# A GRU over 128 steps: the input products of steps 4 to 7 by two-level sums, other load queues, and another order of the program

## The chip, the cores and the metric

One core of a Trainium2 chip runs the whole program. The metric is the device time of one execution in microseconds (us). TensorE (PE) multiplies, VectorE (DVE), ScalarE (ACT) and GpSimd (POOL) do the elementwise work, and SP only issues DMAs; ACT and POOL issue some too.

## The reference

`x` is 64 x 128 x 512 (batch, steps, inputs), `h` is 64 x 512, all in float32. The output is `x` plus the hidden state of each step.

```python
def step(h, inp):
    x_t, prop = inp
    comb = jnp.concatenate([x_t, h], axis=-1)
    z = jax.nn.sigmoid(comb @ Wz + bz)
    r = jax.nn.sigmoid(comb @ Wr + br)
    comb2 = jnp.concatenate([x_t, r * h], axis=-1)
    h_cand = jnp.tanh(comb2 @ Wh + bh)
    h_new = (1.0 - z) * h + z * h_cand
    h_next = jnp.where(prop, jnp.tanh(h_new @ Wp + bp), h_new)
    return (h_next, h_new)
```

`prop` holds in every fourth step (t = 3, 7, ...) but the last. `Wz`, `Wr` and `Wh` are 1024 x 512: the upper half meets x (called the input half, `wx` in the kernel), the lower half meets h (`wh`). `Wp` is 512 x 512 (`wp`).

## The kernel before

The products with h must wait for h, step by step. The products with x don't: they are made ahead, in groups of four steps (group g holds steps 4g to 4g + 3), and fill PE between the products with h. Their results lie as `cp` and are added to, or copied (the line's name is a seed) into, the accumulators of a step.

*Plain products.* `plain(t)` makes the x products of steps 0 to 3. A unit is 8 products of 32 rows by 128 columns for one gate (R, Z, H) and one of the four blocks k of the inputs; there are 48. The profile counts two records for a float32 product, so that a unit is 16 records.

*Batches.* For groups 1 and up `batch(...)` makes the x products by a scheme with seven products instead of eight. A unit is 4 products of 32 x 192 (8 records). The scheme is used on two levels: the outer level has seven products, numbered 1 to 7, each made of seven inner ones (49 units a group), and needs sums of the weights (`tt`, `tw`, `tf`: `sum_inner`, `sum_outer`, all through `weigh`, 128 x 384 on POOL or 128 x 768 on DVE), sums of x between steps and input halves (`o12`, `o34`, made from the transposed x, `xT`), sums of these (`s12r`, `s4r`, `s56`, `s73`, by `four`), and, after the products, folds on POOL (`to_c`, `to_m`, `more_c`: 128 x 768 into `st` or `mb`), whose result goes by a DMA and a copy on ACT into `cp`. A batch holds two of the outer products and uses the scratch banks q, y, a and x; ACT seeds ps_q with the summed bias (`bias_s`, made on POOL) and copies banks into each other; DVE adds two blocks.

Group 1 (steps 4 to 7) is made in another way before: its outer level is an ordinary product (`special`, and `TERMS` for batches that add up two of them), 56 units in three batches, four folds; its sums of x are `s12r` and, by `sum_raw34`, the raw sums of steps 6 and 7, in the buffer of `s73`.

*Recurrent products.* `gates_plain` (steps 0, 1 and 124 to 127) multiplies h with `wh` as it is; `gates_seven` (the others) uses a seven-product scheme with sums `sa` of the transposed h, made on POOL as soon as both halves of h are there (`hT`). Then comes the candidate (products of `rhT`, the transposed r * h, with `wh_2`, into ps_e for one half of the batch and ps_r for the other), and in steps with `prop` the product with `wp`.

*Start.* PE runs 42 products of zeros (`idle`) while the first data are loaded, then the biases are spread over the partitions by products with a row of ones (`spread`, `spread_wide`). SP's queue loads x of step 0, the input halves of Wr, Wz, Wh, x of steps 4 to 7, then `wh` and `wp`. POOL's queue loads x of steps 1 to 3 and h0.

*Order.* Every operation is written into a plan with the data that it reads and writes; the table `ORDER` (a packed list) fixes the order in which the program is emitted, for all engines (`arrange`). An engine does its operations strictly in this order.

## Time and profile before

| | us |
|---|---|
| median of 3 runs | 1230.0 (1229.81 to 1231.96) |
| profiled execution, span | 1229.9 |
| PE busy | 1213.1 |
| POOL, DVE, ACT busy | 942.4, 864.0, 789.1 |
| first x product on PE begins | 9.30 |
| step 0's first product with h begins | 29.25 |
| step 4's first product with h begins | 87.75 |
| step 124's first product with h begins | 1200.45 |
| last product on PE begins | 1223.95 |

Rows of the profile read: start and length in us, engine, line of the kernel, operation, output <- input as the program names them, then sizes and the count; in square brackets the idle time of the engine ahead of the row and what ended it. `s` stands for `s73` or `s56`, `o` for `o12` or `o34`. A row's length on PE holds the way through the array too, so the distance of starts is what a product costs PE.

### The profile page before, as it was taken

To read this page: it belongs to the slowest core of one execution; us is meant where nothing else is said; L and a number is where in the kernel's file an instruction comes from. 1 tells how busy PE (TensorE), PEld (TensorE's weight loads), DVE (VectorE), ACT (ScalarE), POOL (GpSimd) and SP (SyncE) were. 2 spreads that over 40 slices of the span, in tenths; PEclk is the share of its full clock that TensorE was granted. 3 is DMA by queue.
4 is the path that set the end of the run, shared out by engine and by line. 5 is a ranking of instruction groups with operands and counts; after the bars stand their busy time and mean duration, and the time that the engine had idled before them with its cause. 6 is when DMAs were issued, how large, how long until landed. Compare 5 with 4: busy or idle time off the path is not lost.

```text
span 1229.9 us, 85504 instructions
## 1 busy us (share of the span) xinstructions
PE 1213.1 (99%) x37666; PEld 1139.7 (93%) x37666; DVE 864.0 (70%) x2831; ACT 789.1 (64%) x2305; POOL 942.4 (77%) x1489
## 2 busy tenths in 40 slices
...
GB/s 191 128 46 54 39 62 50 59 61 48 54 49 53 60 59 53 40 61 49 64 60 39 55 54 54 64 42 56 50 56 58 60 42 51 57 55 59 39 58 37
DMA packets 92754, 71.50 MB, mean 58 GB/s; under 512 B 7515, under 2 KB 88283, under 8 KB 92382
## 3 DMA queue, kind: packets, MB, share of 16 engines
...
q0 software_dynamic: 512, 0.53, 0.2%
q14 instruction: 76, 0.62, 0.2%
...
## 4 chain that ended last, share of the span: by engine, by line
PE 95%; DMA 2%; SPq 1%; issue 1%; DVE 1%; ACT 0%; POOL 0%; POOLq 0%; ACTq 0%; DVEq 0%
PE ps_e L412 16%; PE ps_r L412 16%; PE ps_b L412 13%; PE ps_y L412 12%; PE ps_q L412 12%; PE ps_x L412 12%; PE ps_z L412 10%; PE ps_a L412 6%; DMA wx<-in_L_cond_Wr_dram 0%; DMA wx<-in_L_cond_Wh_dram 0%; DMA wx<-in_L_cond_Wz_dram 0%; SPq L483 0%; DMA wh<-in_L_cond_Wr_dram 0%; SPq L538 0%; POOL st L860 0%
## 5 line engine op out<-in xcount | busy, mean ns | idle before, releaser
L1070 POOL TENSOR_TENSOR sa<-hT 128x64 f32<-128x64 f32 x244 | 76.3, 322 | 145.4 <-DVE hT L975 92.0
L412 PE MATMUL ps_z<-wh,sa 128*32 128x128 f32 x3904 | 160.8, 273 | 0.9 <-POOL sa L1070 0.9
L860 POOL TENSOR_TENSOR st<-mb,mb 128x768 f32<-128x768 f32 x77 | 141.1, 1833 | 23.0 <-ACT mb L827 18.6
L884 ACT COPY cp<-st 64x384 f32<-64x384 f32 x248 | 125.9, 509 | 25.0 <-DVE keep L1078 11.5
L412 PE MATMUL ps_e<-wh,rhT 128*32 128x128 f32 x4096 | 141.1, 273 | 0.3 <-issue 0.3
L412 PE MATMUL ps_r<-wh,rhT 128*32 128x128 f32 x4096 | 140.4, 273 | 0.7 <-DVE rhT L975 0.6
L412 PEld LDWEIGHTS ps_z<-wh,sa 128*32 128x32 f32 x3904 | 122.5, 110 | 8.7 <-issue 2.4
L412 PEld LDWEIGHTS ps_r<-wh,rhT 128*32 128x32 f32 x4096 | 121.1, 110 | 4.6 <-DVE rhT L975 1.2
L1164 POOL TENSOR_TENSOR xj<-xj,h 128x256 f32<-128x256 f32 x127 | 93.3, 735 | 40.6 <-DVE h L1147 40.3
L412 PEld LDWEIGHTS ps_e<-wh,rhT 128*32 128x32 f32 x4096 | 120.9, 110 | 2.6 <-issue 0.8
L975 DVE STREAM_TRANSPOSE hT<-h 128x128 f32<-128x128 f32 x318 | 98.0, 310 | 34.5 <-ACT h L1022 21.0
L860 POOL TENSOR_TENSOR mb<-mb,mb 128x768 f32<-128x768 f32 x60 | 110.1, 1834 | 13.0 <-ACT mb L827 12.4
L1018 ACT COPY ps_r<-cp 128x128 f32<-128x128 f32 x256 | 69.1, 270 | 56.2 <-DVE h L1147 26.5
L566 DVE STREAM_TRANSPOSE xT<-xj 128x256 f32<-128x256 f32 x128 | 83.4, 655 | 18.2 <-DMA xj<-in_x_dram 11.6
L412 PE MATMUL ps_y<-tw,s 128*32 128x192 f32 x1456 | 94.3, 326 | 0.3 <-issue 0.3
L1078 DVE TENSOR_TENSOR ps_z<-ps_z,keep 128x128 f32<-128x128 f32 x244 | 71.6, 294 | 27.4 <-PE ps_z L412 21.3
L412 PE MATMUL ps_e<-wh,hT 128*32 128x128 f32 x2144 | 86.7, 273 | 1.9 <-ACT ps_e L1018 1.8
L1078 DVE TENSOR_TENSOR keep<-ps_b,cp 128x128 f32<-128x128 f32 x244 | 67.9, 281 | 28.2 <-PE ps_b L412 27.5
L860 POOL TENSOR_TENSOR st<-mb 128x768 f32<-128x768 f32 x47 | 86.1, 1832 | 1.7 <-ACT mb L827 1.0
L1070 POOL TENSOR_TENSOR sa<-hT,sa 128x64 f32<-128x64 f32 x244 | 78.9, 323 | 9.3
L975 DVE STREAM_TRANSPOSE rhT<-rh 128x128 f32<-128x128 f32 x256 | 78.9, 309 | 6.8
L412 PE MATMUL ps_b<-wh,hT 128*32 128x128 f32 x1952 | 80.3, 273 | 0.0
...
## 6 DMA issues: line engine op xcount, KB each, us to landing
...
out_dram<-xj SPq DMA_DIRECT2D x254, 64.0 KB
xj<-in_x_dram SPq DMA_DIRECT2D x248, 64.0 KB
...
```

The source lines that it names most:

```text
L412: nc.tensor.matmul(dst, lhsT=lhsT, rhs=rhs, start=start, stop=True, skip_group_check=True)
L566: lambda: nc.vector.transpose(out=xT_(g)[:, i].rearrange("p c (a h b) -> p h (c a) b", a=S, h=S), in_=xj(t).rearrange("p h (e k) -> p h k ...
L860: el("pool", 768, lambda: nc.gpsimd.tensor_add(dst, a, b), reads, writes, rank=FOLD)
L884: el("act", 384, lambda h=h, own=own: nc.scalar.copy(cp_(2 * g + a)[own, nb, h].rearrange("p b g u -> p (b g u)"), st_(n)[own, h].rearrang ...
L975: add("dve", 0.23, lambda: nc.vector.transpose(out=dst, in_=src), reads, writes, land=0.08, main=True)
L1018: el("act", n, lambda: nc.scalar.copy(dst, src), reads, writes, "+" + bank, main=True)
L1070: tensor(lambda: nc.gpsimd.tensor_sub(sa[:, n], a, b), reads, [("sa", t, n)], n=64, engine="pool")
L1078: tensor(lambda: nc.vector.tensor_add(dst, a, b), reads, writes, used_)
L1164: el("pool", 256, lambda: nc.gpsimd.tensor_add(x_out, x_out, h_(new_)), [("h", new_, 0), ("h", new_, 1)] + xk_, xk_)
```

## The change

Six edits in one:

1. Group 1 is made as the other groups are: 49 units in four batches, (1, 2), (6, 5), (7, 3) and (4) alone, with `s12r`, `o12`, `s56`, `o34`, `s73`, `s4r` and seven folds. `special`, `TERMS` and `sum_raw34` go. The inner weight sums 6, 7 and 4 stand ahead of the batches. A batch may hold one product (W = 1).
2. In `plain`, R and Z of blocks k = 1 to 3 are made by one unit with 256 columns; k = 0 stays apart, since it opens a bank.
3. `wx` is loaded by block and gate in the order R0, Z0, R1, Z1, R2, Z2, R3, Z3, H0 to H3 (one DMA each for k = 0 and 1 of R and Z, two for the others).
4. x of steps 1 to 3 goes from POOL's queue (12 DMAs) to ACT's (6), x of steps 4 to 7 from SP's (8 DMAs between Wh's input half and `wh`) to POOL's (8).
5. In the last group the batch (3, 5) comes before (7, 4); before it was (7, 5), then (3, 4).
6. The table is new.

The diff, cut to its core, with two lines of the table:

```diff
@@ ORDER @@
 ORDER = """
-c-mEYcYIaXneE>D?0tIg_uO;ty~1`J+llR%xFzv;;xxxjb?juEHuENBGMOavUXq!~v;;Lokpu`N5CTLIh>i-95CTN+2+?~-G=b<{p!bRSy+7VvXMNvV>-)
...
+c-n2-2Y40NnK0lv(|ez}Q|`>%izGlagB>T1<HYgWj#HgD#mR2gNgn&zB>V4fc9Y#d+0FBBR)`{j=pdO65+IsDAV8vvCPW8;D57^n6}^}Lo4LXz&(523&Ue0Z
...
@@ -449,28 +427,21 @@
     def rows(ap, t, h):
         return ap[ts(h, V), t, :].rearrange("b (q j) -> q b j", q=NQ)
 
-    def load_x(t):
+    def load_x(t, name="sp"):
         for h in range(S):
-            op = load("sp", lambda h=h: nc.sync.dma_start(out=xj(t)[:, h, :], in_=rows(x, t, h)),
-                      [("xj", t, h, q) for q in range(NQ)], cost=0.585, few=True)
-            if t < 3 * Q4:
+            op = load(name, lambda h=h: queue(name).dma_start(out=xj(t)[:, h, :], in_=rows(x, t, h)),
+                      [("xj", t, h, q) for q in range(NQ)], cost=0.585 if name == "sp" else 0.45, few=True)
+            if 2 * Q4 <= t < 3 * Q4:
                 plan.behind.append((late, op.index))
 
-    def load_wx(i, k, wide=False):
+    def load_wx(i, k, pieces=1):
 
         w = gates_in[i][:D].rearrange("(p k) n -> p k n", k=K)
-        if wide:
-            load("sp", lambda: nc.sync.dma_start(out=wx[:, k, i, :], in_=w[:, k]),
-                 [("wx", 0, i, k)], size=256.0, cost=0.43)
-            return
...
+        tall = P // pieces
+        for n in range(pieces):
+            load("sp", lambda n=n: nc.sync.dma_start(out=wx[ts(n, tall), k, i, :], in_=w[ts(n, tall), k]),
+                 [("wx", 0, i, k, n)], size=256.0 / pieces, cost=0.43)
+        plan.whole(("wx", 0, i, k), [("wx", 0, i, k, n) for n in range(pieces)])
 
     def load_wh(dst, w, keys, over=(), ks=K):
 
@@ -498,46 +469,41 @@
     add("pool", 0.2, lambda: nc.gpsimd.memset(ones, 1.0), (), [("ones", 0)])
     for q in range(NQ):
         load_step(0, q, ("sp", "actq")[q % 2])
+    load_wx(R, 0)
+    load_x(1, "actq")
+    load_wx(Z, 0)
+    load_wx(R, 1)
+    load_x(2, "actq")
+    load_wx(Z, 1)
+    load_x(3, "actq")
     for i in range(3):
         load_bias(i)
-    for i in range(3):
-        for k in range(0, K, 2):
-            if i == R and k == 0:
-                load_wx(i, k, True)
-                load_wx(i, k + 1, True)
-            else:
-                load_wx(i, k)
+    for k in (2, 3):
+        for i in (R, Z):
+            load_wx(i, k, 2)
+    for k in range(K):
+        load_wx(H_, k, 2)
     add(
         "act", 1.5, lambda: nc.scalar.activation(dummy, ones[:, 0:1], AF.Sigmoid),
         [("ones", 0)], [("dummy", 0), ("row_free", 0)],
     )
-    for q in range(NQ):
-        load_step(1, q, "poolq")
-    for h in range(S):
-        for q in range(NQ):
-            load(
-                "poolq",
-                lambda h=h, q=q: nc.gpsimd.dma_start(
-                    out=steps_in[part(q), 2:4, h, :], in_=x[ts(h, V), 2:4, ts(q, J)]),
-                [("xj", t, h, q) for t in (2, 3)], size=32.0,
-            )
     for q in range(NQ):
         load(
             "poolq",
             lambda q=q: nc.gpsimd.dma_start(
                 out=h_(0)[part(q)], in_=h0[:, ts(q, J)].rearrange("(h b) j -> b h j", h=S)
             ),
-            [("h", 0, h, q) for h in range(S)], size=32.0,
+            [("h", 0, h, q) for h in range(S)], [("wx", 0, R, 1)], size=32.0,
         )
     for h in range(S):
         plan.whole(("h", 0, h), [("h", 0, h, q) for q in range(NQ)])
     for h in range(S):
         for q in range(NQ):
             load(
-                "sp",
-                lambda h=h, q=q: nc.sync.dma_start(
+                "poolq",
+                lambda h=h, q=q: nc.gpsimd.dma_start(
                     out=steps_in[part(q), Q4 : 2 * Q4, h, :], in_=x[ts(h, V), Q4 : 2 * Q4, ts(q, J)]),
-                [("xj", t, h, q) for t in range(Q4, 2 * Q4)], cost=0.47,
+                [("xj", t, h, q) for t in range(Q4, 2 * Q4)], [("wx", 0, Z, 2)], size=64.0,
             )
     for i in range(3):
         load_wh(wh[i], gates_in[i][D:], ("wh", 0, i))
@@ -740,37 +702,48 @@
-            for k in range(K):
...
-                def unit(e=e, k=k, ps=ps, slot=slot, c0=c0, s0=s0, first=first):
...
+        def products(k, gates):
...
+            def unit():
+                for h in range(S):
+                    for q in range(NQ):
+                        left = v[:, c0, s0 * B + h * V : s0 * B + (h + 1) * V]
+                        if len(gates) > 1:
+                            mm(ps[part(q), h::2], left, wx[:, k, gates[0] : gates[-1] + 1, ts(q, J)], first and h == 0)
+                        else:
+                            mm(ps[part(q), slot + h], left, wx[:, k, gates[0], ts(q, J)], first and h == 0)
...
+        products(0, [R])
+        products(0, [Z])
+        for k in range(1, K):
+            products(k, [R, Z])
+        for k in range(K):
+            products(k, [H_])
@@ -787,15 +760,16 @@
-        ps = halves
-        mb, c5, q2 = mb_(n), c5_(n), q2_(n)
+        W = len(ms)
+        ps = {b: v[:, :W] for b, v in halves.items()}
+        mb, c5, q2 = mb_(n)[:, :W], c5_(n)[:, :W], q2_(n)[:, :W]
...
-                for x_, w_ in TERMS.get(i, ((i, i),)):
-                    left, lk = lhs(g, x_, j)
-                    right, rk = factor(w_, j)
...
+                left, lk = lhs(g, i, j)
+                right, rk = factor(i, j)
...
@@ -1167,22 +1140,15 @@
             load("sp", lambda h=h: nc.sync.dma_start(out=rows(out, t, h), in_=x_out[:, h, :]),
                  [], [("xj", t, h, q) for q in range(NQ)], cost=0.585, few=True)
 
-    def special(g, a, p1, p2, p3):
-        to_c(g, a, 0, p1, p2)
-        to_c(g, a, 1, p1, p3)
-
     def sums_of(g, *at):
         plan.due = min(at) - 0.3
         for t in range(g * Q4, g * Q4 + Q4):
             join(t)
         plan.due = at[0]
         sum_raw12(g)
-        if g == 1:
-            sum_raw34(g)
-        else:
-            for due, f in zip(at[1:], (sum_s12, sum_s34, sum_raw4)):
-                plan.due = due
-                f(g)
+        for due, f in zip(at[1:], (sum_s12, sum_s34, sum_raw4)):
+            plan.due = due
+            f(g)
 
     add("pe", 0.01, lambda: None, [("bits", 0)],
         [("A", 0), ("R", 0), ("P", 0, 0), ("P", 0, 1)]
@@ -1203,15 +1169,21 @@
     sum_inner(3)
     plan.due = -0.5
     sum_outer()
-    sums_of(1, -1.0)
+    for i in (6, 7, 4):
+        plan.due = -0.4
+        sum_inner(i)
+    sums_of(1, -1.0, -0.9, -0.8, -0.7)
     batch([(1, 1), (1, 2)], 0.0, 0.8, (1, 0))
-    batch([(1, 10), (1, 11)], 0.8, 1.6, (5, 5))
-    batch([(1, 8), (1, 9)], 2.4, 0.8, (1, 0))
-    special(1, 0, 1, 2, 10)
-    special(1, 1, 8, 9, 11)
-    for due, i in ((0.5, 6), (1.0, 7), (1.5, 4)):
-        plan.due = due
-        sum_inner(i)
+    to_c(1, 0, 0, 1, 2)
+    batch([(1, 6), (1, 5)], 0.8, 0.8, (0, 5))
+    to_m(1, 6, 1)
+    n = to_c(1, 0, 1, 6, 5, True)
+    batch([(1, 7), (1, 3)], 1.6, 0.8)
+    more_c(1, 0, 1, n, 3)
+    to_m(1, 7, 6)
+    to_c(1, 1, 1, 7, 5)
+    batch([(1, 4)], 2.4, 0.4)
+    to_c(1, 1, 0, 7, 4)
 
     for k in range(KH):
         b11, b21, b12, b22 = wh[R][:, k], wh[R][:, KH + k], wh[Z][:, k], wh[Z][:, KH + k]
@@ -1246,13 +1218,22 @@
         batch([(o, 2), (o, 6)], at + 4 * L, L)
         to_c(o, 0, 0, 1, 2)
         to_m(o, 6, 1)
-        batch([(o, 7), (o, 5)], at + 5 * L, L, (0, 5))
-        n = to_c(o, 0, 1, 6, 5, True)
-        to_m(o, 7, 6)
-        to_c(o, 1, 1, 7, 5)
-        batch([(o, 3), (o, 4)], at + 6 * L, L)
-        more_c(o, 0, 1, n, 3)
-        to_c(o, 1, 0, 7, 4)
+        if o < T // Q4 - 1:
+            batch([(o, 7), (o, 5)], at + 5 * L, L, (0, 5))
+            n = to_c(o, 0, 1, 6, 5, True)
+            to_m(o, 7, 6)
+            to_c(o, 1, 1, 7, 5)
+            batch([(o, 3), (o, 4)], at + 6 * L, L)
+            more_c(o, 0, 1, n, 3)
+            to_c(o, 1, 0, 7, 4)
+        else:
+            batch([(o, 3), (o, 5)], at + 5 * L, L, (0, 5))
+            n = to_c(o, 0, 1, 6, 5, True)
+            more_c(o, 0, 1, n, 3)
+            batch([(o, 7), (o, 4)], at + 6 * L, L)
+            to_m(o, 7, 6)
+            to_c(o, 1, 1, 7, 5)
+            to_c(o, 1, 0, 7, 4)
 
     plan.due = LAST - 1.0
     load_wh(wz, Wz[D:], ("wz", 0), [("tw", 0, 5, 0), ("tw", 0, 5, 1), ("t5", 0, 5)], KH)
```

The lines of the profile move with it: a product is L412 before and L390 after, a weight sum L611 and L577, a fold L860 and L833, `sa` L1070 and L1043, a transpose of x L566 and L532, a bank copy or seed of a batch L827 and L800, the spreads L925 and L945 to L898 and L918, sums by `four` L643 to L646 to L609 to L612.

What the table does at three places (without the rows' numbers; names carry buffer numbers). PE's first products with x, behind the products of zeros; before:

```order
L925 MATMUL ps_y_114<-wt_68 32x128 x12
L412 MATMUL ps_x_113<-wx_63,xT_0_81 32x128 x8
L412 MATMUL ps_a_112<-wx_63,xT_0_81 32x128 x16
L412 MATMUL ps_x_113<-wx_63,xT_0_81 32x128 x16
L412 MATMUL ps_a_112<-wx_63,xT_0_81 32x128 x16
L412 MATMUL ps_z_107<-wx_63,xT_0_81 32x128 x8
```

and after:

```order
L390 MATMUL ps_b_108<-wx_63,xT_0_81 32x128 x8
L390 MATMUL ps_z_107<-wx_63,xT_0_81 32x128 x8
L390 MATMUL ps_b_108<-wx_63,xT_0_81 32x128 x8
L390 MATMUL ps_z_107<-wx_63,xT_0_81 32x128 x8
L390 MATMUL ps_z_107<-wx_63,xT_0_81 32x2x128 x8
L390 MATMUL ps_a_112<-wx_63,xT_0_81 32x2x128 x8
L390 MATMUL ps_x_113<-wx_63,xT_0_81 32x2x128 x8
L390 MATMUL ps_b_108<-wx_63,xT_0_81 32x2x128 x8
L898 MATMUL ps_y_114<-wt_68 32x128 x12
```

The spread of the biases (from `wt`) moves from the head of the x products behind the first 16 units' worth of them, four merged pairs (2x128) among these.

POOL up to the end of `s73`; before:

```order
L611 TENSOR_TENSOR tw_3_70<-tw_3_70 128x12x32
L1164 TENSOR_TENSOR xj_80<-xj_80,h_1_99 128x256
L643 TENSOR_TENSOR s73_0_93<-xT_1_82 128x128
L644 TENSOR_TENSOR s73_0_93<-s73_0_93,xT_1_82 128x128
L645 TENSOR_TENSOR s73_0_93<-xT_1_82 128x128
L611 TENSOR_TENSOR tt_76<-tt_76,tw_4_71 128x384
L646 TENSOR_TENSOR s73_0_93<-xT_1_82,s73_0_93 128x128
L670 TENSOR_TENSOR o12_0_96<-xT_0_81 128x256
L860 TENSOR_TENSOR st_0_88<-mb_0_85 128x2x2x192
```

and after:

```order
L646 TENSOR_TENSOR o34_0_97<-xT_1_82,o12_0_96 128x256
L1137 TENSOR_TENSOR xj_80<-xj_80,h_1_99 128x256
L577 TENSOR_TENSOR tf_3_75<-wx_63 128x384
L612 TENSOR_TENSOR s56_0_94<-o12_0_96,s56_0_94 128x128
L609 TENSOR_TENSOR s73_0_93<-o34_0_97 128x128
L612 TENSOR_TENSOR s4r_0_95<-xT_1_82,s4r_0_95 128x64
L577 TENSOR_TENSOR tt_76<-tt_76,wx_63 128x384
L833 TENSOR_TENSOR st_0_88<-mb_0_85 128x2x2x192
L577 TENSOR_TENSOR tt_76<-tt_76,tw_4_71 128x384
L611 TENSOR_TENSOR s73_0_93<-o34_0_97 128x128
L610 TENSOR_TENSOR s73_0_93<-s73_0_93,o34_0_97 128x128
L612 TENSOR_TENSOR s73_0_93<-o34_0_97,s73_0_93 128x128
```

The sums of `s73` now come from `o34`, itself a sum, and stand behind `s56`, `s4r` and the first fold into `st`.

PE at the end of step 123; before:

```order
L412 MATMUL ps_z_107<-wh_1_65,sa_0_106 32x128 x8
L412 MATMUL ps_e_109<-wh_2_66,rhT_0_103 32x128 x16
L412 MATMUL ps_z_107<-wh_1_65,sa_0_106 32x128 x8
L412 MATMUL ps_r_110<-wh_2_66,rhT_0_103 32x128 x16
L412 MATMUL ps_e_109<-wp_67,hT_0_100 32x128 x16
L412 MATMUL ps_r_110<-wp_67,hT_0_100 32x128 x16
```

and after:

```order
L390 MATMUL ps_z_107<-wh_1_65,sa_0_106 32x128 x8
L390 MATMUL ps_e_109<-wh_2_66,rhT_0_103 32x128 x16
L390 MATMUL ps_r_110<-wh_2_66,rhT_0_103 32x128 x16
L390 MATMUL ps_y_114<-tw_4_71,s4r_0_95 32x192 x4
L390 MATMUL ps_x_113<-tt_76,o34_0_97 32x192 x4
L390 MATMUL ps_x_113<-tt_76,xT_1_82 32x192 x4
L390 MATMUL ps_e_109<-wp_67,hT_0_100 32x128 x16
L390 MATMUL ps_r_110<-wp_67,hT_0_100 32x128 x16
```

Three batch units stand between the last products of `rhT` and the product with `wp`, and the product with `sa` is ahead of both products of `rhT`.

332 lines of the change are left out of this document (148 added, 184 removed).

## The prediction

> **What bounds the kernel now.** I read the page first, then a table of stages, then single engines where that table shows idle time. From the page, the busy times and the shares of the chain that ended last:
>
> ```profile
> PE 1213.1 (99%) x37666; PEld 1139.7 (93%) x37666; DVE 864.0 (70%) x2831; ACT 789.1 (64%) x2305; POOL 942.4 (77%) x1489
> PE 95%; DMA 2%; SPq 1%; issue 1%; DVE 1%; ACT 0%; POOL 0%; POOLq 0%; ACTq 0%; DVEq 0%
> ```
>
> PE is busy for all but 1229.9 − 1213.1 = 16.8 us of the span. Where those lie is told by PE's busy time in each stretch (columns: stretch, its length, busy time and records, clock, DMA share, GB/s):
>
> ```profile
> 0.00:40.00 40.00, 34.77 (x906) 1.00 0.79 199
> 40.00:60.00 20.00, 19.99 (x600) 1.00 0.30 86
> 60.00:80.00 20.00, 17.88 (x506) 1.00 0.12 31
> 80.00:1150.00 1070.00, 1068.91 (x33351) 1.00 0.21 54
> 1150.00:1200.00 50.00, 48.69 (x1558) 1.00 0.20 53
> 1200.00:1230.00 30.00, 22.82 (x788) 0.99 0.13 34
> ```
>
> From 80 to 1150 us only 1.1 us is idle: the change leaves the work of that stretch alone, so it can neither gain nor lose there. What it can move is the head (5.2 us idle before 40), two stalls between 60 and 80 (2.1), and the last 80 us (8.5). PE's timeline of the head and of those stalls, in order of time:
>
> ```profile
> 6.00 1.69 PE L925 MATMUL ps_y<-wt 1*32 1x128 f32 x24
> 9.30 1.08 PE L412 MATMUL ps_x<-wx,xT 128*32 128x128 f32 x16 [1.61 <-DVE xT L566]
> 10.15 1.93 PE L412 MATMUL ps_a<-wx,xT 128*32 128x128 f32 x32
> 11.86 1.94 PE L412 MATMUL ps_x<-wx,xT 128*32 128x128 f32 x32
> 13.56 1.28 PE L412 MATMUL ps_a<-wx,xT 128*32 128x128 f32 x32
> 14.96 0.64 PE L412 MATMUL ps_z<-wx,xT 128*32 128x128 f32 x16
> ...
> 16.73 1.06 PE L412 MATMUL ps_a<-wx,xT 128*32 128x128 f32 x32
> 17.60 0.62 PE L412 MATMUL ps_x<-wx,xT 128*32 128x128 f32 x16
> ...
> 29.25 0.64 PE L412 MATMUL ps_r<-wh,hT 128*32 128x128 f32 x16
> 30.13 0.64 PE L412 MATMUL ps_r<-wh,hT 128*32 128x128 f32 x16 [0.24 <-DMA wh<-in_L_cond_Wr_dram]
> ...
> 41.11 0.83 PE L412 MATMUL ps_q<-wx,xT 128*32 128x192 f32 x16
> ...
> 57.31 0.83 PE L412 MATMUL ps_q<-tt,s 128*32 128x192 f32 x16
> ...
> 58.29 0.51 PE L412 MATMUL ps_y<-wx,s12r 128*32 128x192 f32 x8
> 58.61 0.51 PE L412 MATMUL ps_y<-tw,s 128*32 128x192 f32 x8
> ...
> 70.66 0.65 PE L412 MATMUL ps_z<-wh,sa 128*32 128x128 f32 x16 [0.85 <-POOL sa L1070]
> ...
> 73.88 0.86 PE L412 MATMUL ps_q<-tt,s12r 128*32 128x192 f32 x16 [1.26 <-ACT ps_a L827]
> ...
> 85.54 1.06 PE L412 MATMUL ps_e<-wp,hT 128*32 128x128 f32 x32
> ```
>
> Starts give the prices, since a duration holds the pipeline too. A plain unit (16 records of 128) costs 0.435 us at full rate (16.73 to 17.60 for two); a batch unit (8 records of 192) 0.32, the 326 ns of the page's records of that size. The seven units from 9.30 to 14.96 took 5.66 us instead of 3.05: PE ran at about half rate there, 2.6 us lost, although the column of the clock says 1.00.
>
> **Units.** Group 1 needs 49 batch units instead of 56: 7 × 0.326 = −2.3 us of PE. Merging R and Z turns 24 plain units (0.435) into 12 of the same 32 records: 0, at most −0.2 of overhead. The one batch more, of half size, costs ACT and DVE some copies beside PE: 0, since both are busy for 64% and 70%; its three more folds are POOL's (3 × 1.84, below). The −2.3 is a gain only while PE has something ready, so the question is who feeds it.
>
> **POOL.** Its timeline, and two of DVE's sums:
>
> ```profile
> 18.21 1.77 POOL L611 TENSOR_TENSOR tf<-wx 128x384 f32<-128x384 f32 x1 [6.59 <-DMA wx<-in_L_cond_Wh_dram]
> ...
> 35.22 0.34 POOL L959 COPY bias_s<-st 128x192 f32<-128x192 f32 x1
> ...
> 40.88 1.00 POOL L611 TENSOR_TENSOR tt<-tw 128x384 f32<-128x384 f32 x1
> ...
> 53.64 0.46 POOL L646 TENSOR_TENSOR s<-xT,s 128x128 f32<-128x128 f32 x1
> 55.56 0.73 POOL L670 TENSOR_TENSOR o<-xT 128x256 f32<-128x256 f32 x1 [1.47 <-DVE xT L566]
> 56.25 1.84 POOL L860 TENSOR_TENSOR st<-mb 128x768 f32<-128x768 f32 x1
> 58.04 0.32 POOL L643 TENSOR_TENSOR s4r<-xT 128x64 f32<-128x64 f32 x1
> ```
>
> ```profile
> 18.16 0.96 DVE L611 TENSOR_TENSOR tw<-wx 128x768 f32<-128x768 f32 x1 [0.69 <-DMA wx<-in_L_cond_Wh_dram]
> ...
> 23.36 1.75 DVE L611 TENSOR_TENSOR tw<-tw,wx 128x768 f32<-128x768 f32 x1
> ```
>
> POOL can begin only when Wh's input half has landed, at 18.2. It then works without a break to 54.1, where the last sum of s73 ends; PE uses s73 at 57.31 (the view writes s for it), so POOL has 3.2 us to spare and is no bound. A weight sum (384 wide) costs 1.00 us alone, but the twelve between 18.21 and 35.22 took 17.0 us, 1.42 each, while DVE ran its own: both engines stretch. All rows to 54.1, priced alone (22 weight sums, 8 sums of 128, one of 256, 2.9 us of bias sums), are 29.3 us; they took 35.9, 35.4 without a wait of 0.5: a ratio of 1.21.
>
> The Trainium skill ("SBUF — State Buffer", section "SBUF: two separate sides") says that VectorE with two SBUF inputs and GpSimd hold a shared port pair as an exclusive lock, the loser blocked for the whole instruction. The 1.00 against 1.42 us agrees in direction. By a pure lock each of the 14 weight sums up to the second mark below would last 1.00 + 0.96 = 1.96 us (an estimate by that page) instead of the 1.42 and 1.21 used there, 8.6 us more and 1235.6 in all; the measured ratios already hold such blocking, so the sum goes by them, and that end lies beyond rival C.
>
> After, s73 is a sum of sums, and more stands ahead of it. By POOL's order there are, up to the second part of s73 (the last that the second step's products take there): 21 weight sums (21.0), 11 sums of 128 (0.46 each, 5.1), 5 of 256 (0.73, 3.7), 4 of 64 (0.32, 1.3), the bias sums (2.9) and one fold (1.84): 35.8 us alone, 6.5 more than before. Its start stays at 18.2: the pieces of Wh's input half still come last, with 0.5 MB of x of steps 4 to 7 beside them from POOL's queue (16.5 if these wait, 19 if they take their share). PE's marks along POOL's order, with units counted from PE's order:
>
> - The bias, which seeds the first batch product: 9 weight sums, 2 of 128 and the bias sums, 12.8 us alone, × 1.42 = 18.2, so 36.4. PE gets there after 21.4 us of units, some 2 of bias spreads and up to 2.6 of half rate; begun at 6.1 (below) it waits from 31 or 32. Wait 4 to 5.
> - o12, second part: 5 weight sums, 2 of 128, 2 of 64, 2 of 256, 8.0 us, × 1.21 = 9.7: 46.1. PE: 36.4 + 7.0 of units = 43.4. Wait 2.7.
> - s73, second part: the other 15.0 us, × 1.13 (a choice between 1.21 and 1.00, since DVE's weight sums are mostly over by then) = 16.9: 63.0. PE: 46.1 + 14.6 of units = 60.7. Wait 2.3.
>
> At 63.0 PE has 1146.0 us of units left. Before, it had 1152.0 left at 57.31 and ran without idle, thus 1146.0 at 63.3. So of the 2.3 us saved and of the head start (next part) only 0.3 is left, 0.8 if the wait ends 0.5 sooner: I take −0.5.
>
> **The loads.** Before, the bias spread goes first (6.00, 1.69 busy), and the first x product at 9.30 waits 1.61 us for the transpose of x. After, PE starts with R and Z of k = 0, which are loaded first, and x of step 0, and the spread comes later: PE goes on at about 6.1, 3.2 earlier, and saves up to 2.6 more where the half rate ends sooner. (It asks for x of step 1 after one unit and for steps 2 and 3 after four and five, so part of the 3.2 can go to their transposes.) It has 43 plain units' records ahead of the first wh product instead of 33 (10 × 0.435 = 4.4 us), and that product cannot be later than before by much: 4 to 5 us of work ahead at 29. By the marks above the wait for POOL takes it away: 0 in the sum, −4 if POOL is faster (rival A). SP's queue loses this row:
>
> ```profile
> 16.55 4.98 SPq L538 DMA_DIRECT2D xj<-in_x_dram x8
> ```
>
> so Wh, R part (second group at 30.13, 0.24 us late) is issued up to 5 us sooner: −0.2 at most, hidden behind the wait for POOL. POOL's queue issues the eight instead, in its idle 6.59 us before 18.21; ACT issues six for steps 1 to 3 where it has nothing ready; both 0, +1 at most if the issues on POOL run past 18.2, since everything above shifts with it.
>
> **Between 63 and 90.** POOL then still has four folds and the sums of group 2 to make up; before, it has room at the end of this stretch:
>
> ```profile
> 85.92 0.73 POOL L1164 TENSOR_TENSOR xj<-xj,h 128x256 f32<-128x256 f32 x1 [3.39 <-DVE h L1147]
> 88.44 0.32 POOL L1070 TENSOR_TENSOR sa<-hT 128x64 f32<-128x64 f32 x1 [1.79 <-PE ps_b L412]
> ```
>
> The two stalls of 0.85 and 1.26 us: the sums sa stand earlier in POOL's order, and ps_a is seeded for other products: −2.1. Late next: sa of step 3 behind three folds of 1.84 in a row on POOL, and sa of step 2 behind s73 (two sums of 0.46 and two of 0.32 against 1.1 us of PE): +0.7, between 0 (queue caught up) and +2.5 (one fold and a half uncovered). By the order PE has 61.2 us of units behind it at the first wp product, 64.9 before; with 63.0 + 18.3 + 0.7 = 82.0 against 85.54, less 1.3 of units that are still to come, the head comes to −2.2; the same by terms is −0.5 − 2.1 + 0.7 = −1.9. I take −2.1.
>
> **The end.** PE's waits there:
>
> ```profile
> 1196.81 1.08 PE L412 MATMUL ps_r<-wh,rhT 128*32 128x128 f32 x32 [0.62 <-DVE rhT L975]
> 1198.58 1.08 PE L412 MATMUL ps_e<-wp,hT 128*32 128x128 f32 x32 [0.69 <-DVE hT L975]
> 1206.59 1.08 PE L412 MATMUL ps_e<-wh,hT 128*32 128x128 f32 x32 [0.69 <-ACT ps_e L1018]
> ```
>
> Three batch units (0.98) now stand between step 123's rhT products and wp: the 0.69 is filled, −0.7. Those units' folds and copies come later by that, but serve steps 126 and 127, 9 us on: 0. z ahead of r in steps 125 to 127 leaves only one product group (0.87) instead of 1.3 between r and its rhT product: up to +0.4 a step, taken back where the next step's wait shrinks by as much; I take −0.1 in all (z is ready earlier), −0.6 to +0.9. End: −0.8.
>
> **Sum.** −2.1 − 0.8 = −2.9 against the profiled 1229.9, which is 0.1 under the median 1230.0: 1227.0 us.
>
> **Rivals.**
>
> A. *POOL keeps up.* At alone prices s73 would be there at 18.2 + 35.8 = 54.0, and PE's own pace would rule. Before, PE needed 57.31 − 9.30 = 48.0 us for 39.3 us of units, 8.7 over; after, with the same and 0.7 for the moved spread, it has 42.9 us done at 6.1 + 42.9 + 9.4 = 58.4, 4.6 ahead of the forecast's 63.0: 1222.4. For it: the sum at 40.88 ran at 1.00. Against: the 1.42 ahead of 35. Chance 0.17.
>
> B. *PE is slowed by its own waits.* Before, an idle 1.61 us was followed by half rate for 4.7 us, at a price of 2.6 us. After has waits of 4 to 5, 3 and 2.3 us. What follows the first two is swallowed by the next wait; what follows the third is not: 1227.0 + 2.6 = 1229.6, no change. The 0.85 and 1.26 us idles speak against (the rows behind 73.88 run at full pace). Chance 0.18.
> The Trainium skill ("TensorE: Matmul & The Clock Gate", "Part 1: The HAM clock gate") has the array fall to half rate after an idle window of about 3.4 us and need as long a busy one. By that rule only the first wait would do it, and the time would be 1227.0; the trace's stretch to 14 us agrees with a slow start.
>
> C. *Slower: POOL stretched throughout.* If the ratio 1.42 of the first 17 us holds to the end of s73 (DVE then has more transposes of x earlier), that end is 18.2 + 35.8 × 1.42 = 69.0, 6.0 late: 1233.0. It decides from 65.9 (gain gone); at 68.5 the kernel is slower by over 0.2%. Chance 0.18.
>
> Forecast as worked out: 0.47, own range 1225 to 1229.
>
> **How the numbers follow.** 0.2% (2.5 us) is about what a measurement of this kernel tells from no change: faster means under 1227.5, slower over 1232.5. Faster: three quarters of 0.47 and A: 0.52. Slower: half of C, and starts or waits at their upper ends: 0.17. The same: 0.31. Range from A to just short of C: 1222.2 to 1232.5.
>
> **What would show it.** Right: the first wx product near 6; PE waits of over 2 us released by POOL or by ACT's seeds between 31 and 64; POOL busy without a break from 18 to past 63; no stalls of 0.85 and 1.26 us after; no 0.69 ahead of wp. Wrong: POOL starting after 19 or before 16; the last s73 sum before 58 (A) or after 66 (C); rows at half pace behind a wait (B); new waits in steps 4 to 8 from a POOL that is still late, which the sum holds at 0 because of the 3.39 and 1.79 us above.

## The result and the profile after

The changed kernel took 1247.5 us, the median of four runs (1246.1 to 1251.5), against 1230.4 for the kernel before (1229.8 to 1232.0): a ratio of 1.014 with a 95% interval of 1.0121 to 1.0159. It is 17 us slower; 1227.0 was forecast, with a range that ended at 1232.5. The profiled execution is the slowest of the four, 1251.5 us with a span of 1249.6, so its stages add up to 19.7 us of loss, 2.6 more than the medians differ.

From the page of the changed kernel, the busy times and the shares of the chain that ended last:

```profile
PE 1219.3 (98%) x37418; PEld 1120.6 (90%) x37418; DVE 870.5 (70%) x2833; ACT 776.1 (62%) x2309; POOL 954.7 (76%) x1500
PE 87%; DVE 3%; POOL 3%; DMA 2%; ACT 2%; issue 1%; SPq 1%; ACTq 0%; DVEq 0%; POOLq 0%
```

PE's share of the chain fell from 95% to 87%, with every other engine in it for a few per cent. PE by stage (columns as before):

```profile
0.00:40.00 40.00, 29.61 (x626) 0.91 0.67 189
40.00:60.00 20.00, 15.06 (x384) 0.91 0.36 86
60.00:80.00 20.00, 19.82 (x612) 1.00 0.04 10
80.00:1150.00 1070.00, 1064.00 (x32920) 1.00 0.21 53
```

The head now idles 10.4 us before 40 instead of 5.2, and 4.9 between 40 and 60 where it idled for nothing. In the long stretch from 80 to 1150 only 6.0 us of idle shows. That number hides most of what happens there, since a product's row holds its pipeline too and a gap of a few tenths disappears under it. The starts show it: PE's product with `wp`, made every fourth step, is a clock for the whole run. Its rows in steps 3 and 7, after:

```profile
89.61 1.08 PE L390 MATMUL ps_e<-wp,hT 128*32 128x128 f32 x32
129.55 1.08 PE L390 MATMUL ps_e<-wp,hT 128*32 128x128 f32 x32
```

The start of the same product in all kernels that matter, in us (the last column is the span; the kernels from the third on are experiments, told below):

| kernel | step 3 | step 7 | step 123 | step 7 to 123 | end |
|---|---|---|---|---|---|
| before | 85.5 | 122.7 | 1198.6 | 1075.9 | 1229.9 |
| after | 89.6 | 129.6 | 1216.2 | 1086.7 | 1249.6 |
| x1to3_on_pool | 84.2 | 127.0 | 1215.2 | 1088.2 | 1249.0 |
| old_steady_order | 89.3 | 131.4 | 1207.0 | 1075.6 | 1238.0 |
| old_steady_x_on_pool | 83.9 | 127.0 | 1207.6 | 1080.6 | 1238.3 |
| new_steady_order | 84.9 | 122.0 | 1209.0 | 1087.1 | 1242.5 |
| new_tail | 85.3 | 122.4 | 1198.6 | 1076.2 | 1232.1 |

Read by its first two rows, the change lost 4.1 us up to step 3, 2.8 more to step 7, 10.8 from there to step 123, and 2.0 in the end: 19.7 in all. Each row is one execution. How much one can stray in the long stretch is shown by the four rows with the order of before there: three have 1075.6 to 1076.2 us, old_steady_x_on_pool, the slowest of its four runs, has 1080.6. The three rows with the new order, 1086.7 to 1088.2, lie clear of that.

**The head.** PE's first two rows with x, POOL's first sum and DVE's transpose of x of step 1, all of the changed kernel:

```profile
5.61 1.09 PE L390 MATMUL ps_a<-wx,xT 128*32 128x128 f32 x16
12.37 1.94 PE L390 MATMUL ps_x<-wx,xT 128*32 128x128 f32 x32 [5.67 <-DVE xT L532]
```

```profile
23.88 1.79 POOL L577 TENSOR_TENSOR tf<-wx 128x384 f32<-128x384 f32 x1 [12.53 <-DMA wx<-in_L_cond_Wh_dram]
```

```profile
11.68 0.63 DVE L532 STREAM_TRANSPOSE xT<-xj 128x256 f32<-128x256 f32 x1 [7.32 <-DMA xj<-in_x_dram]
```

PE does begin with x early, at 5.61 where 6.1 was forecast (the order listed for it in "The change" starts four units later than that). But one unit on it needs x of step 1, which DVE gets only at 11.68. And POOL's first weight sum is not at 18.2 but at 23.88. The first comes from ACT's queue itself: it issues x of step 1 from 1.69 us on (below), and DVE gets it some 10 us later; from POOL's queue in experiment 1 DVE gets it at 7.65. Why it takes longer from ACT's is not shown.

```profile
1.69 1.71 ACTq L432 DMA_DIRECT2D xj<-in_x_dram  x2
```

The reason for POOL's late start stands in SP's queue (the waits of SP before 50 us, and where its eight loads of Wh's input half begin; after, then before):

```profile
SPq L442 <- DMA xj<-in_x_dram: 9.8, 3, 3.8
19.20 5.40 SPq L442 DMA_DIRECT2D wx<-in_L_cond_Wh_dram  x8
```

```profile
SPq L469 <- DMA xj<-in_x_dram: 0.9, 1, 0.9
11.41 4.70 SPq L469 DMA_DIRECT2D wx<-in_L_cond_Wh_dram  x8
```

SP spends 9.8 us waiting for loads of x that ACT issued. In the built program the DMAs of SP's and of ACT's queues count on the same eight semaphores in turn (POOL's queue has eight of its own), and a DMA waits until the one that used its semaphore before has landed. So the weight loads in SP's queue stand still for an x load of ACT's (below, the third DMA waits for the semaphore that the second has taken):

```
ACT: L432 DMA xj<-in_x_dram 128x1x128 [waits DMAHW2_49]
ACT: L432 DMA xj<-in_x_dram 128x1x128 [waits DMAHW3_49]
SP:  L442 DMA wx<-in_L_cond_Wz_dram 64x512 [waits DMAHW3_49]
SP:  L442 DMA wx<-in_L_cond_Wr_dram 64x512 [waits DMAHW5_49]
```

**The long stretch.** Between 110 and 1190 us PE's listed waits are 0.9 us before and 3.8 after. To see the rest, take the start of each group of PE's records, subtract the start of the group before and that group's records at PE's full rate (0.0272 us for one of 128 columns, 0.0407 for one of 192; records that the trace lacks are made up to whole units), and count gaps of 0.05 us and more: 53 gaps with 7.1 us in all before, 104 with 16.4 after. The new order stops PE nowhere for more than 0.9 us; it makes it wait in twice as many places. About half of what is added lies in gaps of over 0.25 us (6 with 2.2 us before, 14 with 7.3 after), the rest in shorter ones that a list of waits hardly shows.

### The profile page after: what moved, and what is told of

The parts are those of the page before. It is cut to its first block, busy times and chain, and to the rows that moved or that the text cites. A ratio compares the mean times of both kernels' runs of the same rounds, so it can differ in the third digit from the quotient of the medians.

```text
span 1249.6 us, 85087 instructions
## 1 busy us (share of the span) xinstructions
PE 1219.3 (98%) x37418; PEld 1120.6 (90%) x37418; DVE 870.5 (70%) x2833; ACT 776.1 (62%) x2309; POOL 954.7 (76%) x1500
## 3 DMA queue, kind: packets, MB, share of 16 engines
q1 hardware_dynamic: 90328, 64.84, 19.7%
q10 hardware_dynamic: 1150, 0.53, 0.2%
## 4 chain that ended last, share of the span: by engine, by line
PE 87%; DVE 3%; POOL 3%; DMA 2%; ACT 2%; issue 1%; SPq 1%; ACTq 0%; DVEq 0%; POOLq 0%
PE ps_r L390 15%; PE ps_e L390 15%; PE ps_b L390 12%; PE ps_q L390 11%; PE ps_y L390 11%; PE ps_x L390 10%; PE ps_z L390 9%; PE ps_a L390 5%; DMA cp<-st 1%; POOL st L833 1%; DMA xj<-in_x_dram 1%; SPq L442 1%; DMA wx<-in_L_cond_Wr_dram 0%; POOL tt L577 0%; ACT cp L857 0%
## 5 line engine op out<-in xcount | busy, mean ns | idle before, releaser
L1043 POOL TENSOR_TENSOR sa<-hT 128x64 f32<-128x64 f32 x244 | 76.9, 322 | 116.6 <-DVE hT L948 82.1
L390 PE MATMUL ps_z<-wh,sa 128*32 128x128 f32 x3904 | 160.1, 273 | 1.3 <-POOL sa L1043 1.3
L833 POOL TENSOR_TENSOR st<-mb,mb 128x768 f32<-128x768 f32 x77 | 141.0, 1832 | 23.3 <-DVE ps_e L1106 4.8
L390 PE MATMUL ps_r<-wh,rhT 128*32 128x128 f32 x4096 | 140.3, 273 | 2.4 <-DVE rhT L948 2.0
L390 PE MATMUL ps_e<-wh,rhT 128*32 128x128 f32 x4096 | 141.2, 274 | 0.2 <-DVE rhT L948 0.2
L390 PEld LDWEIGHTS ps_z<-wh,sa 128*32 128x32 f32 x3904 | 119.1, 110 | 12.8 <-issue 3.2
L390 PEld LDWEIGHTS ps_r<-wh,rhT 128*32 128x32 f32 x4096 | 119.5, 110 | 8.0 <-DVE rhT L948 3.1
L833 POOL TENSOR_TENSOR mb<-mb,mb 128x768 f32<-128x768 f32 x62 | 113.7, 1833 | 14.0 <-ACT mb L800 8.7
L390 PEld LDWEIGHTS ps_e<-wh,rhT 128*32 128x32 f32 x4096 | 120.2, 110 | 2.8 <-DVE rhT L948 0.7
L833 POOL TENSOR_TENSOR st<-mb 128x768 f32<-128x768 f32 x47 | 86.1, 1834 | 9.7 <-ACT cp L857 3.7
L532 DVE STREAM_TRANSPOSE xT<-xj 128x256 f32<-128x256 f32 x128 | 82.3, 654 | 15.3 <-DMA xj<-in_x_dram 15.1
L390 PE MATMUL ps_y<-tw,s 128*32 128x192 f32 x1488 | 91.2, 326 | 0.0
L390 PE MATMUL ps_e<-wh,hT 128*32 128x128 f32 x2144 | 87.1, 274 | 2.6 <-DVE hT L948 1.2
L1009 DVE TENSOR_TENSOR rh<-ps_e,h 128x128 f32<-128x128 f32 x128 | 36.7, 287 | 74.5 <-ACT ps_e L995 72.7
L1043 POOL TENSOR_TENSOR sa<-hT,sa 128x64 f32<-128x64 f32 x244 | 78.5, 322 | 13.1
```

Of the source, the lines that this page charges most:

```text
L390: nc.tensor.matmul(dst, lhsT=lhsT, rhs=rhs, start=start, stop=True, skip_group_check=True)
L532: lambda: nc.vector.transpose(out=xT_(g)[:, i].rearrange("p c (a h b) -> p h (c a) b", a=S, h=S), in_=xj(t).rearrange("p h (e k) -> p h k ...
L833: el("pool", 768, lambda: nc.gpsimd.tensor_add(dst, a, b), reads, writes, rank=FOLD)
L1009: tensor(lambda: nc.vector.tensor_mul(rh_(t)[:, h, :], ps, h_(v)[:, h, :]), [(name, 0), ("h", v, h)], [("rh", t, h)], bank)
L1043: tensor(lambda: nc.gpsimd.tensor_sub(sa[:, n], a, b), reads, [("sa", t, n)], n=64, engine="pool")
```

## The experiments

**1. x of steps 1 to 3 on POOL's queue (x1to3_on_pool).** The changed kernel, with its own order:

```diff
-    load_x(1, "actq")
+    load_x(1, "poolq")
...
-    load_x(2, "actq")
+    load_x(2, "poolq")
...
-    load_x(3, "actq")
+    load_x(3, "poolq")
```

> The changed kernel with one edit: x of steps 1 to 3 (six DMAs of 64 KB) is issued by POOL's queue ahead of h0 instead of by ACT's; order and all else stay. In the changed kernel's trace SP's queue waited 9.8 us in three pieces for DMAs of x before it could issue the input halves of the weights, and Wh's arrived at 23.8 us instead of 18.2. Theory S (SP is held up by the completion of ACT's slow DMAs, and POOL, DVE and PE then start later): those waits are gone, POOL's first weight sum starts at 17 to 20 us, and the time falls by 3 to 6 us to 1242 to 1245. Rival D (the DMA engines are simply full, and it doesn't matter which queue x is on): POOL's first sum stays at 22 to 24, the time at 1246 to 1249.

It took 1248.9 us (1246.1 to 1251.1), ratio 1.0138 [1.0113, 1.0163]: no gain at all, where 3 to 6 us were expected. Yet the start behaves as it should. SP's wait for x, and POOL's first sum:

```profile
SPq L442 <- DMA xj<-in_x_dram: 1.0, 1, 1.0
18.43 1.77 POOL L577 TENSOR_TENSOR tf<-wx 128x384 f32<-128x384 f32 x1 [3.51 <-DMA wx<-in_L_cond_Wh_dram]
102.63 0.64 PE L390 MATMUL ps_z<-wh,sa 128*32 128x128 f32 x16 [2.43 <-POOL sa L1043]
```

The mechanism at the start is shown: with the x loads on POOL's queue the weight loads come 5.4 us sooner, and step 3's `wp` product stands at 84.2, 5.4 ahead of the change and 1.3 ahead of the kernel before. By step 7 it is 4.3 behind the kernel before, 5.6 lost on the way. The last row is one place where: PE waits 2.43 us for POOL's `sa`. The clock that PE is granted is then 0.58 from 103 to 107 us, about 1.7 us more (an estimate, (1 − 0.58) × 4), and about 1.0 us is only work that stood ahead of step 3 before. From step 7 on the stretch costs 12.3 us more than before. The start was not what decided.

**2. The order of before from step 5 on (old_steady_order).** The changed program, its table taken from the change up to `rhT` of step 5 and from the kernel before behind that; the last group's batches as before:

```diff
@@ ORDER @@
-(all rows in the order of the change)
+(up to rhT of step 5 the order of the change, from there that of the kernel before)
@@ last group @@
-        if o < T // Q4 - 1:
+        if True:
```

> The changed kernel, its own order up to the middle of step 5 and from there the order of the kernel before (the last group's batches as before too). Theory O (about 12 of the 17 us are lost from step 4 to 123 because the new order leaves products a little too close behind what they need, in waits each too short for the profile to list): time per four steps falls from 37.6 to 37.1, the time to 1233 to 1237, some 2 of it at the end. Rival L (the loss after step 4 comes from the late start, POOL never catching up): no change by the order, 1245 to 1249.

1241.5 us (1239.7 to 1242.2), ratio 1.0083 [1.0068, 1.0098]: 6.0 back by the medians, less than theory O had and more than rival L. The stretch from step 7 to 123 takes 1075.6 us, as before (1075.9), so the long stretch's loss is gone. What remains, 11 us by the medians and 8.1 in the trace (the fastest of the four runs), is already there at step 7, so it arises in the head.

**3. The changed order alone (new_steady_order).** The reverse: the kernel before up to `rhT` of step 5, the change's order (and its last group) from there on. Head, loads, group 1 and PE's products are those of before.

```diff
@@ ORDER @@
-(all rows in the order of the kernel before)
+(up to rhT of step 5 that order, from there the order of the change)
@@ last group @@
+        if o < T // Q4 - 1:
...
+            batch([(o, 3), (o, 5)], at + 5 * L, L, (0, 5))
```

> The kernel before, its own order up to the middle of step 5 and from there the order of the changed kernel (with the last group's batches as in the change). Theory O: 12 us over the steps and 2 at the end are lost without any of the other edits, 1241 to 1246. Rival L: within 3 us of the kernel before, 1228 to 1233.

1243.6 us (1242.6 to 1244.3), ratio 1.0102 [1.0087, 1.0117]. The reordering by itself, with the last group's batches in it, costs 12.8 us, with no edit to the loads, the weights or group 1. Where the time goes can be read from the engines behind PE. Waits between 110 and 1190 us (engine and line, what it waited for, us in total, times, longest), before and then this kernel:

```profile
DVE rh L1036 <- ACT ps_e L1022: 49.2, 73, 1.9
DVE hT L975 <- ACT h L1022: 18.7, 38, 1.1
POOL st L860 <- DMA cp<-st: 1.0, 1, 1.0
SPq L454 <- DMA out_dram<-xj: 107.5, 131, 2.4
```

```profile
DVE rh L1009 <- ACT ps_e L995: 66.1, 72, 2.1
DVE hT L948 <- ACT h L995: 28.5, 45, 2.0
POOL st L833 <- DMA cp<-st: 12.3, 7, 3.1
SPq L427 <- DMA out_dram<-xj: 169.9, 93, 4.0
```

The recurrence's own chain (gate on ACT, `rh` or `h` on DVE, transpose, product) waits longer at both of DVE's stations, POOL's folds wait for copies by DMA, and SP's loads of x wait longer for the stores ahead of them. (The folds' waits for ACT get shorter at the same time; all their waits together go from 34.0 to 48.8 us.) Two of the few gaps that are long enough to be listed show how such a lateness reaches PE. DVE, held up by an x load, makes `ps_z` late; and a fold that waited stands ahead of `sa` in POOL's queue:

```profile
995.99 1.23 DVE L539 STREAM_TRANSPOSE xT<-xj 128x256 f32<-128x256 f32 x2 [1.30 <-DMA xj<-in_x_dram]
998.86 0.65 PE L385 MATMUL ps_z<-wh,sa 128*32 128x128 f32 x16 [1.15 <-DVE ps_z L1051]
```

```profile
658.89 1.82 POOL L833 TENSOR_TENSOR st<-mb,mb 128x768 f32<-128x768 f32 x1 [5.38 <-ACT ps_x L800]
660.66 0.32 POOL L1043 TENSOR_TENSOR sa<-hT 128x64 f32<-128x64 f32 x1
661.04 0.64 PE L385 MATMUL ps_b<-wx,sa 128*32 128x128 f32 x16 [1.15 <-POOL sa L1043]
```

Counted as above there are 100 gaps with 18.1 us (before: 53 with 7.1); the 11.0 us between them agrees with the 11.2 of step 7 to 123. Listed as waits are 5.3 us of it (before 0.9).

**4. Both repairs (old_steady_x_on_pool).** Experiment 2 with x of steps 1 to 3 on POOL's queue.

```diff
@@ old_steady_order @@
-    load_x(1, "actq")
+    load_x(1, "poolq")
...
```

> Both edits of the first two kernels of this call in one. If theories S and O both hold and add up, 1228 to 1233, about the kernel before. If only one holds, 1235 to 1245. What the two-level sums of steps 4 to 7 are worth would be seen here against the kernel before: by the prediction's sum up to 2.3 us of PE are saved, and POOL's sums come as late as it said.

1237.5 us (1236.7 to 1240.2), ratio 1.0056 [1.004, 1.0073]: the start's part is another 4.0. Still 6.7 above the kernel before. In the trace 4.3 of it are there at step 7 (127.0 against 122.7), lost between steps 3 and 7; the 4.7 more from there to step 123 come in an execution 2.7 us slower than the median, and no run says what they are. Between steps 3 and 7 POOL is the late one:

```profile
99.15 1.81 POOL L844 TENSOR_TENSOR st<-mb 128x768 f32<-128x768 f32 x1 [2.12 <-DMA cp<-st]
101.29 0.65 PE L401 MATMUL ps_z<-wh,sa 128*32 128x128 f32 x16 [1.45 <-POOL sa L1054]
111.34 0.65 PE L401 MATMUL ps_b<-wt,sa 128*32 128x128 f32 x16 [1.73 <-DVE cand L1062]
```

A fold waits 2.12 us for the copy that it adds to, with `sa` behind it, and PE waits for `sa`. The last row stands just behind the place where the two orders are joined. Experiment 2 has such a wait there too (1.38 us), the kernel before and the change have none, so up to 1.7 us of the loss can be the joint's.

**5 and 6. The two moves of x by themselves.** In the kernel before, with its order: the twelve DMAs of steps 1 to 3 from POOL's queue to ACT's, and the eight of steps 4 to 7 from SP's to POOL's.

```diff
@@ before_x1to3_on_act @@
-        load_step(1, q, "poolq")
+        load_step(1, q, "actq")
...
-                "poolq",
-                lambda h=h, q=q: nc.gpsimd.dma_start(
+                "actq",
+                lambda h=h, q=q: nc.scalar.dma_start(
@@ before_x4to7_on_pool @@
-                "sp",
-                lambda h=h, q=q: nc.sync.dma_start(
+                "poolq",
+                lambda h=h, q=q: nc.gpsimd.dma_start(
```

> The kernel before with one edit: the twelve DMAs of x of steps 1 to 3 are issued by ACT's queue instead of POOL's; order, loads and all else as before. Theory S (the DMAs of SP and ACT are counted on the same eight counters, so that SP may not issue while an old one of ACT's is unfinished): SP waits for DMAs of x for 3 to 10 us ahead of the input halves, POOL's first weight sum moves from 18.2 to 21 to 26 us, the time rises by 2 to 8 us to 1233 to 1238. Rival (only the changed order of the weights' blocks and the bigger pieces did it): POOL's sum stays within 1 us of 18.2, the time within 1.5 us of the kernel before.

> The kernel before with one edit: the eight DMAs of x of steps 4 to 7 are issued by POOL's queue (behind x of steps 1 to 3 and h0) instead of SP's between Wh's input half and wh. The prediction put this at 0 with +1 at most. If the 5 us of SP's issue time were a cost, wh arrives up to 5 us sooner and the time falls by 0 to 1 us; if POOL's issues run past 18.2 us or the x crowds out the input halves, POOL's sums start 0.5 to 2 us later and up to 2 us are lost: 1229 to 1232.

1234.2 us, ratio 1.003 [1.0018, 1.0042], and 1234.4, ratio 1.0025 [1.0012, 1.0038]: each move costs about 3 us alone, the second more than expected. In the first, SP again waits for x, and POOL begins late:

```profile
SPq L469 <- DMA xj<-in_x_dram: 4.2, 2, 3.8
20.88 1.73 POOL L611 TENSOR_TENSOR tf<-wx 128x384 f32<-128x384 f32 x1 [17.23 <-DMA wx<-in_L_cond_Wh_dram]
```

So the price of the shared semaphores is found in the other kernel too: 4.2 us of waits on SP, 2.7 of POOL's start, 2.7 of time. In the second POOL begins at 19.06 instead of 18.21, and PE waits for its sums; step 3's `wp` product is 1.6 us late, the rest of the loss is not traced:

```profile
19.06 1.75 POOL L611 TENSOR_TENSOR tf<-wx 128x384 f32<-128x384 f32 x1 [6.14 <-DMA wx<-in_L_cond_Wh_dram]
45.62 0.86 PE L412 MATMUL ps_q<-tt,s12r 128*32 128x192 f32 x16 [1.33 <-POOL s12r L644]
```

**7. The end alone (new_tail).** The kernel before, with the change's order and last group from `rhT` of step 110 on.

```diff
@@ ORDER @@
-(all rows in the order of the kernel before)
+(up to rhT of step 110 that order, from there the order of the change)
```

> The kernel before up to step 110, and from there the order of the change, with the last group's batches (3, 5) before (7, 4) and the products for z ahead of those for r. In the changed kernel's trace the stretch from step 123's product with wp to the end is 33.4 us against 31.3. Theory T (the new end costs about 2 us by itself: rhT of the second half is waited for 0.5 us in three steps, and the last output's DMA leaves later): 1231.5 to 1234. Rival (that stretch is only late because of what came before it): 1228.5 to 1231.

1234.1 us, ratio 1.0023 [1.0012, 1.0035]: the end costs about 2.6 where a gain of 0.8 was forecast. Step 123 is on time (1198.6 in both). Behind it PE's waits change places: the 0.69, 0.38 and 0.73 ahead of `ps_e<-wh,hT` shrink to 0.41 and 0.30, and new ones stand ahead of the second product with `rhT`. The last step shows why (this kernel, then before):

```profile
1222.74 1.08 PE L401 MATMUL ps_r<-wh,hT 128*32 128x128 f32 x32
1223.74 0.37 ACT L1011 ACTIVATE ps_z<-ps_z 128x256 f32<-128x256 f32 x1 [1.53 <-DVE ps_z L1047]
1224.02 0.26 ACT L1011 ACTIVATE ps_r<-ps_r 128x128 f32<-128x128 f32 x1
1225.16 1.08 PE L401 MATMUL ps_r<-wh,rhT 128*32 128x128 f32 x32 [0.46 <-DVE rhT L964]
```

```profile
1221.33 1.08 PE L412 MATMUL ps_r<-wh,hT 128*32 128x128 f32 x32
1222.53 0.26 ACT L1022 ACTIVATE ps_r<-ps_r 128x128 f32<-128x128 f32 x1 [1.54 <-PE ps_r L412]
1223.95 1.08 PE L412 MATMUL ps_r<-wh,rhT 128*32 128x128 f32 x32
```

With all products for z ahead of r's on PE, only one product (0.87 us) is left between r's and the one with its `rhT`: from r's start to the other's it is 2.42 us, of which 1.74 are products. Before, it was 2.62 us, filled with products. On ACT z stands ahead of r too, but that costs little: r starts 0.20 us behind its product's end, 0.12 before. The last product starts 1.2 us later than before; the rest, 1.0 us, comes behind the last product: 1232.1 − 1225.2 = 6.9 us to the end against 1229.9 − 1223.95 = 5.95.

**8. The two-level sums alone (two_level_alone): not settled.** The kernel before with group 1 made as in the change. Its order had to be made by machine, rows of the new group 1 being put between rows of before at the places that they have in the change.

```diff
@@ kernel before @@
-    batch([(1, 10), (1, 11)], 0.8, 1.6, (5, 5))
-    batch([(1, 8), (1, 9)], 2.4, 0.8, (1, 0))
+    batch([(1, 6), (1, 5)], 0.8, 0.8, (0, 5))
+    batch([(1, 7), (1, 3)], 1.6, 0.8)
+    batch([(1, 4)], 2.4, 0.4)
```

> The kernel before with one part of the change alone: group 1 by two-level sums (49 units for 56, the extra sums and folds on POOL, the weight sums 6, 7 and 4 ahead), its loads, its separate products for R and Z and the order of all other work as before; the operations of group 1 stand where the change has them between the same products with h. The prediction's marks, with POOL starting at 18.2: waits of PE for o12 and s73 between 42 and 63 us, then a gain of about 2 us, 1228 to 1229.5. If POOL's sums and folds, which come late and in a row, cost more in steps 2 to 8 than the 2.3 us of PE saved, 1231 to 1236. If POOL hides all of it, 1226.5 to 1228.

1269.7 us, ratio 1.0319 [1.0301, 1.0336]. None of the three cases had 38 us, and the trace points at the order that I made. PE's longest wait, with POOL held shortly before:

```profile
PE ps_q L402 <- ACT ps_q L812: 11.7, 1, 11.7
78.18 1.82 POOL L845 TENSOR_TENSOR st<-mb 128x768 f32<-128x768 f32 x1 [7.53 <-ACT mb L812]
```

A fold of group 1 waits 7.53 us for ACT's copy in front of everything else on POOL. What part of the 38 us the order has and what part the sums is not shown, so the run says nothing of the two-level sums' own worth.

**9 and 10. Orders laid out again.** If thin margins are the cause, an order laid out with the delays that the traces show should bring time back, in the whole run (after_reordered) or in the head of experiment 4 (head_reordered).

```diff
@@ ORDER, after_reordered @@
-(the order of the change)
+(the same, but PE, ACT and DVE each take the first of their next 12 or 4 rows that is ready)
@@ ORDER, head_reordered @@
-(the order of old_steady_x_on_pool)
+(the same, but PE, DVE, ACT and POOL laid out again so up to step 10)
```

> The changed kernel, all six edits in place, but with its table laid out again: PE takes, of the next 12 of its instructions by the old table, the first whose operands are there (ACT and DVE of their next 4), where the delays are those of the traces (0.26 us from a product's last record to ACT's or DVE's start, 0.2 back to PE, ACT and DVE instructions 0.02 and 0.03 longer than the kernel's own planner takes them). POOL and SP keep their order. Theory M (thin margins: the new table puts the steps' products so close behind DVE and ACT that many small waits, mostly under 0.25 us, add up to 10 us): more than half of the steady loss comes back, 1234 to 1240, and PE's time from step 3's first wp product to step 123's falls from 1126.6 to under 1121. Rival W (the loss is in the changed work itself, POOL's longer chain and the loads, whatever the order): 1245 to 1250.

> The kernel of old_steady_x_on_pool (the changed head with x of steps 1 to 3 on POOL's queue, from step 5 on the order of before; 1237.5), with the order of PE, DVE, ACT and POOL up to step 10 laid out again by the same rule and the same delays. Theory H (steps 3 to 8 lose 6 to 7 us because sums and folds stand ahead of sa in POOL's queue and PE has nothing else in line): 1229 to 1232, at the level of the kernel before. Rival P (with group 1's sums in two levels POOL has more to do there than the stretch has room for): 1235 to 1238.

1286.1 us, ratio 1.0443 [1.042, 1.0467], and 1240.8, ratio 1.0071 [1.0051, 1.0091]: both slower than what they started from, where theories M and H had a gain of 6 to 13 us. Neither theory gave such times, and they do not choose between M and W. What they do show is how little these two orders, laid out by estimated delays, are worth: the first has 166 gaps with 49.7 us. That taking every instruction as early as the estimate allows leaves nothing between a result and its use would explain it, but is not shown. Whether the loss between steps 3 and 7 can be ordered away stays open for the same reason.

**11 and 12. Longer hops, in both orders.** A test of the margins that needs no new order: every hop of the recurrence gets one more DVE instruction, in the kernel before (before_longer_hops) and in experiment 3 (new_steady_longer_hops).

```diff
-        add("dve", 0.23, lambda: nc.vector.transpose(out=dst, in_=src), reads, writes, land=0.08, main=True)
+        def twice():
+            nc.vector.transpose(out=dst[:, 0:32], in_=src[:, 0:32])
+            nc.vector.transpose(out=dst, in_=src)
+
+        add("dve", 0.23, twice, reads, writes, land=0.08, main=True)
```

> The kernel before, with one more DVE instruction in each hop of the recurrence: ahead of every transpose into hT or rhT (some 510 in all, about 4.2 a step) the first 32 columns are transposed alone, an estimated 0.1 us each. Theory M (the order of before leaves the products more time behind DVE than the new one): part of the longer hop is swallowed by that room; 5 to 20 us more than before, and clearly less than the other kernel of this pair gains. Rival F (the new order loses a fixed amount that has nothing to do with how late DVE is): the same rise in both.

> The kernel of new_steady_order (1243.6: before until step 5, the changed order from there) with the same extra DVE instruction in each hop. Theory M: with less room left each longer hop comes through, so this kernel rises at least 1.4 times as much as the kernel before does with the same edit, and the distance of 12 to 13 us between the two grows to 18 or more. Rival F: the distance stays at 12 to 13 us.

1275.6 us (1274.8 to 1276.2), ratio 1.0357 [1.0338, 1.0376], and 1314.6 (1314.0 to 1315.2), ratio 1.0672 [1.0656, 1.0689]. The kernel before rises by 44.5 us, the one with the new order by 70.9: 1.6 times as much, and the distance between them grows from 12.8 to 39.0. The extra instruction is the same in both, 574 times (318 into `hT`, 256 into `rhT`) and not the some 510 expected, at 0.208 us and not 0.1. Its group for `hT` from 110 to 1190 us in the first kernel (209 ns in the second):

```profile
L976 DVE STREAM_TRANSPOSE hT<-h 128x32 f32<-128x32 f32 x280 | 58.2, 208 | 17.5 <-ACT h L1026 8.4
```

That is what thin margins behind DVE would do, and what a fixed loss would not: rival F is out. Which rows of the table take the room away, these two runs do not tell. The gaps went from 53 to 234 (42.3 us) in the one and from 100 to 296 (75.1) in the other. My size for the kernel before, 5 to 20 us, was too low: it has more room than the new order, not much of it.

## Why the prediction was wrong

**"From 80 to 1150 us only 1.1 us is idle: the change leaves the work of that stretch alone, so it can neither gain nor lose there."** This is the step that failed. It cost 10.8 of the 19.7 us, and experiment 3 has 12.8 from the order alone, some 2.6 of that in the end. A stretch in which PE hardly idles has little to gain, but it can lose, and the table was new for the whole run; the prediction looked at three places of it and held the rest to be unchanged because the work is. The work is the same and its order is not: 53 gaps become 104. Experiments 2 and 3 show that it is the order, 11 and 12 that it leaves the products less room behind DVE; how much ACT, POOL and SP have in it was not separated. The rivals did not have this case either: all three were placed before 70 us.

**The loads: "ACT issues six for steps 1 to 3 where it has nothing ready; both 0, +1 at most".** Wrong by mechanism. ACT was idle, as said, but SP paid: 9.8 us of waits for loads that share its semaphores, and POOL's start at 23.88 instead of 18.2 ("POOL starting after 19" was one of the signs of being wrong). That PE asks for x of step 1 after one unit was seen, but got no price; the wait was 5.67 us. I had counted the issues on each queue and not what the queue behind them would wait for. The price of the loads in the total is 4.0 us with the order of before behind step 5 (experiment 4 against 2) and 2.7 in the kernel before (experiment 5); in the changed kernel itself nothing was won back (experiment 1). Moving x of steps 4 to 7, also held at 0, costs about 3 alone.

**POOL's marks.** Here the working held, but for the start and one wait. From POOL's first sum to the bias, to the second part of `o12` and to the second part of `s73` the forecast had 18.2, 27.9 and 44.8 us. POOL's rows at the three marks of the changed kernel:

```profile
43.33 0.34 POOL L932 COPY bias_s<-st 128x192 f32<-128x192 f32 x1
...
53.27 0.72 POOL L635 TENSOR_TENSOR o<-o,xT 128x256 f32<-128x256 f32 x1
...
69.99 0.46 POOL L610 TENSOR_TENSOR s<-s,o 128x128 f32<-128x128 f32 x1
```

From 23.88 to the ends of these rows that is 19.8, 30.1 and 46.6 us, and with x on POOL's queue, where the sums begin at 18.43, it is 19.9, 30.2 and 46.7: 1.6 to 2.3 us more than forecast. In both traces 2.08 us of it is one wait of POOL for DVE's transpose of x, ahead of the first mark, which the forecast did not have (it said "POOL busy without a break"); without it the ratios of 1.42, 1.21 and 1.13 to the lone durations, read from the kernel before, come within 0.5 us. The Trainium skill ("SBUF — State Buffer", section "SBUF: two separate sides") has an exclusive lock, by which the second mark would have come 8.6 us later than forecast; neither trace shows it. Of PE's three waits at the marks one came as forecast, 2.66 us for the second part of `o12` where 2.7 was said; at the bias it was 1.25 instead of 4 to 5, and at `s73` there was none where 2.3 was said:

```profile
54.05 1.50 PE L390 MATMUL ps_q<-tw,o 128*32 128x192 f32 x16 [2.66 <-POOL o L635]
```

**Units: −2.3.** The work did shrink by that: PE's records fell from 37666 to 37418, at full rate 2.3 us (56 fewer of batch units; merging R and Z takes off 192 more, at no gain, since a merged unit is 16 records of twice the width). As time it is not seen by itself in any run. Without the shared semaphores step 3's `wp` product stands 1.3 us ahead of the kernel before where 3.5 was forecast, and 1.3 us of PE's work stands behind that product now instead of ahead of it, so nothing is gained there. The 2.2 us missing are POOL's: `s73`'s second part ends at 65.1 there (63.0 forecast), and from it to the `wp` product it is 19.2 us where 19.0 was forecast.

**Between 63 and 90: −2.1, then +0.7.** The two stalls did go. What comes in their place is larger than the 0.7: from step 3 to step 7 the loss is 2.8 us in the change and 5.6 where the start is mended, with PE waiting for `sa` behind a fold (2.43 us in experiment 1, 1.45 in 4). "New waits in steps 4 to 8 from a POOL that is still late, which the sum holds at 0" was named as a sign of being wrong, and they came.

**The end: −0.8.** It was +2.0 in the profile and about +2.6 in experiment 7. The 0.69 ahead of `wp` was filled, as forecast. The term that was mis-sized is "z ahead of r": −0.1 was taken, between −0.6 and +0.9, with 1.3 us of products before between r and its `rhT` product where the last step has 1.75. The last product came 1.2 us late, and about 1 us more appears behind it, which was not priced at all.

**Rivals.** None of the three is what happened. A and C are out, since POOL's ratios came as forecast. B's mechanism, slow PE after its own waits, is there: in the changed kernel the clock is 0.50 and 0.68 in the stretches at the 5.67 us wait and 0.57 in the 4 us from the 2.66 us wait on; in experiment 1 (last row) it is 0.57 right behind a 2.17 us wait for `o12` that ends at 48.68 (columns as in the table of stages):

```profile
10.00:14.00 4.00, 1.63 (x32) 0.50 0.53 141
14.00:18.00 4.00, 2.40 (x52) 0.68 0.43 132
54.00:58.00 4.00, 3.95 (x76) 0.57 0.15 46
49.00:53.00 4.00, 4.00 (x88) 0.57 0.13 39
```

In the third of these it costs PE about (1 − 0.57) × 4 = 1.7 us, an estimate, and the starts agree: from 54.05 to 58.14 PE does 2.4 us of work. But PE then comes to `s73` at 70.70, a quarter of a us behind its sum, where a wait of 2.3 was forecast. So this price takes the place of the third wait, as B itself has it for the first two. The Trainium skill ("TensorE: Matmul & The Clock Gate", "Part 1: The HAM clock gate") has the clock fall after an idle window of about 3.4 us; here PE had stood still for 2.66 and 2.17.

**Left open.** The account by medians is 6.7 us for group 1's code and the head's order (experiment 4), 4.0 for the start (2 against 4) and 6.0 for the order behind step 5 (the change against 2). The parts are not fixed prices: the same exchange of the order gives 11.4 with the start mended (1 against 4) and 12.8 counted from the kernel before. The changed kernel's own runs spread over 5.4 us, which can be part of the reason; the rest is not explained. How much of the 6.7 is the two-level sums' POOL work and how much its place in the queue, experiments 8 and 10 do not tell. No kernel here beat the one before.
